# Image loads and stores of a grouped involution in halves, one to a row, behind a wait for VectorE

## The chip, the cores and the metric

The kernel runs on one core of one Trainium2 chip. The metric is the device time of one execution in microseconds (us). Every engine of the core (TensorE, VectorE, ScalarE, GpSimd, SyncE) runs its own stream of instructions in order, and semaphores order them against each other. Nearly all transfers are issued by SyncE (SP in the profile), one after the other, and are carried out by 16 DMA engines.

## The reference, cut to what matters

The input x is 8 images of 256 channels of 56 x 56, all in float32. Layer 0 adds to x an involution of its group norm; layer 1 adds a block of two 3 x 3 convolutions with ternary weights.

```python
def _L0_conv_ref(x, w_reduce, b_reduce, w_span, b_span):
    ker = jnp.einsum('bchw,oc->bohw', x, w_reduce) + b_reduce[None, :, None, None]
    ker = jnp.einsum('bchw,oc->bohw', ker, w_span) + b_span[None, :, None, None]
    ker = ker.reshape(B, G, 1, K * K, H, W)
    ...
    patches = patches.reshape(B, G, C // G, K * K, H, W)
    out = (ker * patches).sum(axis=3)
    return out.reshape(B, C, H, W)

def _L1_conv_ref(x, w1, w2, g1, b1, g2, b2):
    out1 = noised_tri_conv(x, w1)
    out1 = batch_norm_train(out1, g1, b1)
    out1 = jax.nn.relu(out1)
    out2 = noised_tri_conv(out1, w2)
    out2 = batch_norm_train(out2, g2, b2)
    return jax.nn.relu(out1 + out2)

x = x + _L0_conv_ref(_gn(x), L0_conv_w_reduce, L0_conv_b_reduce, L0_conv_w_span, L0_conv_b_span)
x = x + _L1_conv_ref(_gn(x), L1_conv_w1, L1_conv_w2, L1_conv_g1, L1_conv_b1, L1_conv_g2, L1_conv_b2)
return x
```

In layer 0 every pixel has its own 7 x 7 kernel (K = 7) for each of 16 groups of 16 channels (G = 16), and that kernel is a linear function of the pixel's own 256 channels. The change lies in layer 0.

## The kernel before

Three stages follow each other: the involution (layer 0) with its sums stored in DRAM as x1d, the two convolutions by way of y1d and y2d, and a tail that adds up and writes out. The change touches the involution alone.

**Tiling.** An image b is cut into four quarters c of 64 channels. A quarter's image tile `x` has 128 partitions: 64 channels of the upper half of the picture and the same 64 of the lower half, each with 1568 pixels. A quarter is worked on in ten rows of tiles, ty = 0 to 9, three picture rows high (the last one row high). So there are 8 x 4 x 10 = 320 rows; r = 10 c + ty counts the 40 rows of an image, and m counts the 32 quarters.

**A row.** `apply_row` multiplies on TensorE the pixel neighbourhood `q` of the row (a tile of 448 KB, read from DRAM by `load_q`) by the quarter's matrices `a`, in 56 small matmuls (L917; 28 in the last row), into `pa`. ScalarE (L927) and VectorE (L930) pick the wanted part out of it into `inv`, and GpSimd adds `inv` to x (L935). Meanwhile the matrices of the following quarter are made: `generate` yields 14 units of matmuls (L876) whose results VectorE (L890) and ScalarE (L880) move into `a`, and two steps `constant` (L845 on TensorE, L853 on VectorE). `PER_ROW` says how many of these steps a row takes: 2, 2, 2, 1, 2, 2, 2, 2, 1, 0. Rows 24 to 34 also compute the reduced kernels of the following image (`reduce`, L775, from its x tiles), and rows 4 to 18 its statistics (`gn1_stats`, L162). From row 8 of the whole on, up to about row 295, the ternary weights are made by the way: pieces of w are loaded (L319, L244) and stored again (L348, `wqd<-piece_w`) through the same SP.

**Transfers.** SP issues in the order of the text. At the start of a row stands at most one transfer of an image tile: a store of the quarter before in rows 2 and 3 (`store_x1`, L956, 64 partitions x 1568 pixels, 392 KB each), otherwise a load for the following image at the rows of `X_AT` (`load_x`, L666, 128 partitions x 784 pixels, 392 KB). Then, after `apply_row`, `prefetch` loads the `q` of five rows later into the buffer that this row has just read (`NQB` = 5), so that load waits for TensorE. GpSimd fills the rim of a `q` (L813) three rows before it is used. Tiles of x have 2 x 4 - 1 = 7 buffers. A new tile waits until its buffer's earlier tile has been read by all, the store among them.

**Order.** `pin`, at the end of every row, fixes the order of each engine's instructions to that of the text. TensorE's instructions don't change in number or order from row to row by anything said here.

Of the kernel before, what the change touches and what calls it, by code (L numbers as in the profile page):

```python
# [28 lines left out]
CH = P // 2  # L29
# [4 lines left out]
NHW = HH * W  # L34
# [27 lines left out]

PER_ROW = (2, 2, 2, 1, 2, 2, 2, 2, 1, 0)
CONST_AT = 5
NQB = 5
PLEAD = 2
RIM_AT = 1
# [31 lines left out]
def involution_tri_block_kernel(  # L99
# [3 lines left out]
    nc = tc.nc  # L103
# [6 lines left out]
    def scratch(name):  # L110
        return [[dram.tile([P, HW], F32, tag=f"{name}_{b}_{t}", name=f"{name}_{b}_{t}")
                 for t in range(CT)] for b in range(B)]

    x1_d, y1_d, y2_d = scratch("x1d"), scratch("y1d"), scratch("y2d")
# [520 lines left out]
    with ExitStack() as ph1:  # L635
# [22 lines left out]
        work = ph1.enter_context(tc.tile_pool(name="work", bufs=2))  # L658
        apool1 = ph1.enter_context(tc.tile_pool(name="apool1", bufs=1))

        def load_x(b, c, j, queue=nc.sync):

            if j == 0:
                xs[b, c] = xpool.tile([P, NHW], F32, tag="x", name=f"x_{b}_{c}")
            part = slice(j * NHW // 2, (j + 1) * NHW // 2)
            queue.dma_start(xs[b, c][:, part], x[b, c, :, part])  # L666

        def gn1_stats(b, c, j):

            if j == 0:  # L670
                gst1[c] = small.tile([P, NCB, 6], F32, tag="gn_st", name=f"st_{b}_{c}")
                if c == 0:
                    mvs[b] = small.tile([P, NCQ, 2], F32, tag="gn_mv", name=f"mv_{b}")
            image_stats(gst1[c], xs[b, c], j)
            if j == NCB - 1:
                nc.vector.bn_aggr(mvs[b][:, c, :], gst1[c].rearrange("p n s -> p (n s)"))
# [42 lines left out]
        def gn2_params(b0, b1):  # L719

            yield from group_norm_params(
                mv2[:, b0:b1].rearrange("p b t s -> p (b t) s"),
                gn2h[:, b0:b1].rearrange("p b t s -> p (b t) s"), ps_one, f"gn2_{b0}")

            for h in range(2):
                rows = slice(h * CH, (h + 1) * CH)
                nc.vector.tensor_copy(gn2[rows, b0:b1], gn2h[rows, b0:b1, h::2, :])

        gst1, mvs = {}, {}
        prm, xs = {}, {}  # L730
        for c in range(NCQ):
            for j, queue in enumerate((nc.sync, nc.scalar)):
                load_x(0, c, j, queue)
        nc.scalar.dma_start(*later.pop(0))

        def fixed(shape, name, src=None, pool=fix):
# [57 lines left out]
        def rim_of(b, c):  # L794

            sides = work.tile([P, 2, P], F32, tag="sides", name=f"sides_{b}_{c}")
            tops = work.tile([P, 3, CH], F32, tag="tops", name=f"tops_{b}_{c}")
            rim = prm[b][3][:, c]
            for dst, k0, k1, f1 in ((sides, 0, 2, P), (tops, 2, 5, CH)):
                shape = [NQ, k1 - k0, f1]  # L800
                nc.gpsimd.tensor_tensor(dst[:NQ], rims_sb[:NQ, k0:k1].unsqueeze(2).to_broadcast(shape),
                                        rim[:NQ, :f1].unsqueeze(1).to_broadcast(shape), ALU.mult)
            low = work.tile([P, CH], F32, tag="low", name=f"low_{b}_{c}")
            nc.gpsimd.tensor_copy(low[:NQ], rim[:NQ, CH:])
            around[b, c] = sides, tops, low
# [52 lines left out]
        def generate(b, c, a, shared=()):  # L858
# [5 lines left out]
            for u, (gp, p0, n) in enumerate(UNITS):  # L864
# [29 lines left out]
                yield  # L894
                if u == CONST_AT:
                    next(made)
# [3 lines left out]
        def apply_row(b, c, a, ty):  # L900


            ps = ps_a.tile([P, 512], F32, tag="pa", name=f"pa_{b}_{c}_{ty}")
            row_ps[:] = [ps]
            q = loads.pop((b, c, ty))
            whole, rest = views(a)
            if ty < TY - 1:
                av, n, t0, t1 = whole, NP, ty * TX, (TY - 1 + ty) * TX
            else:
                av, n, t0, t1 = rest, PX, 0, TX  # L910
            m = 32 if ty < TY - 1 else CH
            w = n * m * GQ // CH
            for k in range(TX):
                for h, t in enumerate((t0, t1)):
                    for g in range(CH // m):
                        o = h * CH + g * m
                        nc.tensor.matmul(ps[o:o + m, k * w:(k + 1) * w], q[:NQ, k, o:o + m],  # L917
                                         av[:, t + k, g * w:(g + 1) * w], start=True, stop=True)
            return ps, n, w // n
# [18 lines left out]
        queue = [(b, c, ty) for b in range(B) for c in range(NCQ) for ty in range(TY)]  # L938
        loads, bare, filled, around = {}, [], [], {}

        def prefetch():
            if queue:
                k = queue.pop(0)
                loads[k] = load_q(*k)
                bare.append(k)

        def surround(keep=PLEAD):
            for k in filled:
                fill_end(*k)
            filled.clear()  # L950
            while len(bare) > keep or bare and not queue:
                filled.append(bare.pop(0))
                fill_rim(*filled[-1])

        def store_x1(b, c, h):
            nc.sync.dma_start(  # L956
                x1_d[b][c // 2][c % 2 * CH:(c % 2 + 1) * CH, h * NHW:(h + 1) * NHW],
                xs[b, c][h * CH:(h + 1) * CH])

        gst = {}  # L960

        def gn2_stats(b, c, ty):

            if ty == 1:
                gst[b, c] = (small.tile([P, NCB, 6], F32, tag="gn_st2", name=f"st2_{b}_{c}"), 0)
            st, j = gst[b, c]
            while j < NCB and ((j + 1) * NC <= ty * PY * W or ty == TY):
                image_stats(st, xs[b, c], j)
                j += 1
            gst[b, c] = (st, j)  # L970
            if ty == TY:
                nc.vector.bn_aggr(mv2[:, b, c, :], st.rearrange("p n s -> p (n s)"))
# [25 lines left out]
        def matrices(m):  # L998
            return (apool if m % 2 == 0 else apool1).tile(
                [P, A_COLS], F32, tag=f"a{m % 2}", name=f"a_{m}")  # L1000

        held = []
        qpool = ph1.enter_context(tc.tile_pool(name="qpool", bufs=NQB))
        pieces = ph1.enter_context(tc.tile_pool(name="pieces", bufs=1))
# [30 lines left out]
        rim_of(0, 0)  # L1035
        for _ in range(NQB):
            prefetch()
# [9 lines left out]
        quarters = [(b, c) for b in range(B) for c in range(NCQ)]  # L1047


        X_AT = (0, 1, 4, 5, 7, 8, 14, 15)  # L1050
        PARAMS_AT = 20

        QUANT_AT = 8
        rows = [(b, c, ty) for b, c in quarters for ty in range(TY)]
# [5 lines left out]
        last = None  # L1060
        for m, (b, c) in enumerate(quarters):
            a = a_next
            gen = iter(())
            if m + 1 < len(quarters):
                a_next = matrices(m + 1)
                gen = generate(*quarters[m + 1], a_next)
            more = b + 1 < B
            for ty in range(TY):
                r = c * TY + ty

                if last is not None and ty in (2, 3):
                    store_x1(*last, ty - 2)
                elif more and r in X_AT:
                    load_x(b + 1, X_AT.index(r) // 2, X_AT.index(r) % 2)
                row = apply_row(b, c, a, ty)
                prefetch()

                if r == PARAMS_AT:
                    norm = params(b + 1) if more else gn2_params(0, b)
                next(norm, None)  # L1080

                if ty == 1 and last is not None:
                    gn2_stats(*last, TY)
                elif ty >= 2:
                    gn2_stats(b, c, ty - 1)
                for k in STATS_AT.get(r, ()) if more else ():
                    gn1_stats(b + 1, k // NCB, k % NCB)
                pick_out(b, c, ty, *row)
                surround()
                if ty == RIM_AT and m + 1 < len(quarters):  # L1090
                    rim_of(*quarters[m + 1])
                next(norm, None)
                for _ in range(PER_ROW[ty]):
                    next(gen, None)
                if more and r in STRIPS:
                    reduce(b + 1, *STRIPS[r])
                if m * TY + ty >= QUANT_AT:
                    next(quant, None)
                pin()
            for _ in gen:  # L1100
                pass
            last = b, c
# [1 line left out]
            pass  # L1104
        gn2_stats(*last, TY)
        for h in range(2):
            store_x1(*last, h)
        for _ in gn2_params(B - 1, B):
            pass

# [3 lines left out]
    with ExitStack() as ph2:  # L1114
# [36 lines left out]
        _, total = conv_phase(2, begun, y1_d, norm_y1, st2, nc2, y2_d, False, stays)  # L1151
# [4 lines left out]
    with ExitStack() as ph4:  # L1156

        h = [ph4.enter_context(tc.tile_pool(name=f"f{i}", bufs=1)) for i in range(11)]
# [27 lines left out]
        for j in range(B * CT):  # L1186
            b, t = (j // CT - 1) % B, j % CT
            n = parts_of.get(j, 1)
# [99 lines left out]
```

## Time and profile before

| | us |
|---|---|
| median of 3 runs (lowest, highest) | 2114.55 (2106.56, 2117.14) |
| the profiled execution | 2115.09 |
| its span | 2113.3 |
| involution (start to first matmul of L573) | 0 to 1033 |
| the two convolutions (L573) | 1033 to about 1900 |
| tail | about 1900 to 2113 |

Busy time in the whole span: TensorE 1744.4 us (83%), VectorE 1778.7 (84%), ScalarE 1379.2 (65%), GpSimd 463.0 (22%). Between 1100 and 1800 us TensorE is busy without a gap except at the change from the first convolution to the second. The costliest transfers of the involution, from the list of DMA issues: 320 loads of q of 448 KB each, which land a median 4.2 us after the issue; 64 loads of x of 392 KB, 5.0 us (5.4 for the 64 stores x1d of 392 KB); 64 stores of weight pieces of 144 KB, 5.2 us.

How to read the profile: PE is TensorE, PEld its loading of stationary operands, DVE VectorE, ACT ScalarE, POOL GpSimd, SP SyncE. A group names the line, the engine, the operation, out<-in and the tile. After the bar stand the total busy time and the mean in ns of one, then the idle time of the engine just before these instructions and what ended most of it. "issue" means that the profile shows nothing for which the engine waited. Lines of the waits have the total in us, the number of times and the longest one. Lines of the windows have the stretch, its length, busy time of PE, PEld, DVE, ACT and POOL with instruction counts, the granted TensorE clock, the mean busy share of the DMA engines, and GB/s. Lines of the timeline have the start, the length, engine, line and operation, and in brackets the idle time before and what ended it.

### The profile page before, as it was taken

The page shows a single profiled execution, that of the slowest core. Times are in us where ns is not written, and L with a number is a line of the kernel's source. Part 1 is how long each engine was busy: PE and PEld are TensorE (multiplying, and loading weights), DVE is VectorE, ACT ScalarE, POOL GpSimd, SP SyncE. Part 2 cuts the span into 40 slices and gives each one's busy share as a digit, 9 for nine tenths or more (in the row PEclk, how much of TensorE's full clock was granted, in tenths as well). Part 3 has the DMA queues.
Part 4 walks back from the last instruction along what each step waited for, and adds up shares of the span by engine and source line. Part 5 has one row for each costly group of instructions (what it writes and reads, how often), then busy time and mean ns, then how long its engine had stood idle before and what let it go on. Part 6 is the DMA issues. An engine that isn't in the chain of part 4 may idle for free.

```text
span 2113.3 us, 70523 instructions
## 1 busy us (share of the span) xinstructions
PE 1744.4 (83%) x29680; PEld 1612.1 (76%) x29680; DVE 1778.7 (84%) x3488; ACT 1379.2 (65%) x3413; POOL 463.0 (22%) x836
## 2 busy tenths in 40 slices
PE   5898898989889898898699999998999999990000
PEld 5786786867778786777699999998999999990000
DVE  6887879788797978878799999998999999987444
ACT  3776677766767677687467666664566666675343
POOL 1444444444444444455100000000000000000000
PEclk9999999999999999999799999999999999995555
DMA  5767778686777868677733333335234333359999
GB/s 188 226 185 230 212 202 253 185 252 202 252 216 212 244 176 256 192 212 230 269 115 135 124 123 118 124 121 196 94 125 155 125 125 125 125 213 417 430 430 396
DMA packets 154792, 433.62 MB, mean 205 GB/s; under 512 B 62942, under 2 KB 73052, under 8 KB 147564
## 3 DMA queue, kind: packets, MB, share of 16 engines
q1 hardware_dynamic: 149184, 399.08, 56.0%
q10 hardware_dynamic: 5004, 29.95, 3.4%
q8 instruction: 235, 3.85, 0.8%
q14 instruction: 81, 0.66, 0.1%
q0 software_dynamic: 288, 0.08, 0.0%
HBM read 320.07 MB, written 108.99 MB: 203 GB/s over the span
## 4 chain that ended last, share of the span: by engine, by line
PE 71%; DVE 10%; DMA 10%; issue 6%; ACT 3%; POOL 0%; ACTq 0%; SPq 0%; POOLq 0%; DVEq 0%
PE c L573 40%; PE pg L876 16%; PE pa L917 9%; DMA y1f<-y1d 7%; PE pk L775 4%; PE ks L845 2%; ACT a L880 2%; DVE a L890 1%; DMA out_y<-x1f 1%; DVE inv L930 1%; DVE st L162 1%; DVE x L853 1%; DMA wr<-in_w_red 1%; DVE y1f L1198 1%; DMA q<-in_x_nb 1%
## 5 line engine op out<-in xcount | busy, mean ns | idle before, releaser
L573 PE MATMUL c<-pl,wq 128*128 128x392 f32 x4608 | 856.9, 348 | 9.5 <-ACT pl L443 9.2
L573 PEld LDWEIGHTS c<-pl,wq 128*128 128x128 f32 x4608 | 854.9, 190 | 11.2 <-ACT pl L443 9.6
L880 ACT ACTIVATE a<-pg,bt 126x126 f32<-126x126 f32 x2028 | 519.2, 459 | 90.1 <-PE pg L876 87.1
L876 PE MATMUL pg<-kr,wl 64*126 64x140 f32 (+1 forms) x6144 | 447.9, 293 | 22.7 <-issue 17.6
L876 PEld LDWEIGHTS pg<-kr,wl 64*126 64x126 f32 x6144 | 397.4, 197 | 43.0 <-issue 19.0
L917 PEld LDWEIGHTS pa<-a,q 126*32 126x32 f32 x17024 | 237.2, 114 | 164.6 <-issue 105.7
L917 PE MATMUL pa<-a,q 126*32 126x48 f32 x17024 | 286.7, 213 | 78.9 <-issue 72.8
L890 DVE TENSOR_TENSOR a<-pg,bt 126x504 f32<-126x504 f32 (+4 forms) x640 | 278.7, 479 | 40.2 <-PE pg L876 36.8
L935 POOL TENSOR_TENSOR x<-x,inv 128x168 f32<-128x168 f32 x310 | 161.1, 520 | 520.5 <-DVE inv L930 392.1
L927 ACT ACTIVATE inv<-pa,gn1b,gn1s 128x168 f32<-128x168 f32 x320 | 163.6, 511 | 161.5 <-PE pa L917 105.2
L420 ACT CAST pl<-r 128x812 fp32r<-128x812 f32 x190 | 160.8, 867 | 130.9 <-DVE r L415 121.6
L930 DVE SCALAR_TENSOR_TENSOR inv<-pa,gn1s,inv 128x168 f32<-128x168 f32 (+1 forms) x384 | 134.0, 351 | 129.2 <-ACT inv L927 123.8
L813 POOL TENSOR_TENSOR q<-q,sides 126x256 f32<-126x256 f32 (+1 forms) x320 | 225.7, 706 | 7.3 <-DMA q<-in_x_nb 7.3
L421 DVE TENSOR_TENSOR pl<-r,pl 128x812 fp32r<-128x812 f32 x190 | 184.6, 997 | 24.9 <-ACT pl L420 23.4
L501 ACT ACTIVATE dummy<-y,nc 128x1568 f32<-128x1568 f32 (+1 forms) x128 | 200.0, 1562 | 3.0 <-DVE y L593 1.8
L396 POOL MEMSET xp<- 128x116 f32 x32 | 6.3, 197 | 829.6 <-DVE a L415 759.2
L162 DVE BATCH_NORM_STATS2 st<-x 128x6 f32<-128x392 f32 x256 | 136.9, 553 | 7.4 <-DMA x<-in_x 7.4
L1145 ACT ACTIVATE xp<-raw,bi_bn,sc_bn 128x392 f32<-128x392 f32 (+1 forms) x125 | 83.0, 721 | 60.3 <-DVE a L415 58.9
L1125 ACT ACTIVATE xp<-raw,gn 128x392 f32<-128x392 f32 (+1 forms) x125 | 83.1, 720 | 58.9 <-DVE a L415 58.9
L775 PE MATMUL pk<-x,wrn 64*128 64x168 f32 (+1 forms) x1152 | 104.1, 319 | 4.1 <-DVE x L853 2.4
L775 PEld LDWEIGHTS pk<-x,wrn 64*128 64x128 f32 x1152 | 91.5, 192 | 16.2 <-issue 9.1
L1200 DVE TENSOR_TENSOR x1f<-x1f,y1f 128x3136 f32<-128x3136 f32 (+2 forms) x22 | 55.5, 2533 | 44.2 <-DMA x1f<-x1d 37.4
(185 smaller groups left out, 1660.7 us busy)
## 6 DMA issues: line engine op xcount, KB each, us to landing
q<-in_x_nb SPq DMA_DIRECT2D x320, 448.0 KB, 4.2
raw<-x1d SPq DMA_DIRECT2D x32, 812.0 KB, 6.5
raw<-y1d SPq DMA_DIRECT2D x32, 812.0 KB, 7.2
x1d<-x SPq DMA_DIRECT2D x64, 392.0 KB, 5.4
x<-in_x SPq DMA_DIRECT2D x60, 392.0 KB, 5.0
y1d<-y SPq DMA_DIRECT2D x30, 784.0 KB, 3.3
y2d<-y SPq DMA_DIRECT2D x28, 784.0 KB, 4.0
x1f<-x1d SPq DMA_DIRECT2D x14, 1568.0 KB, 29.3
```

The costliest lines, as they stand in the source:

```text
L420: nc.scalar.copy(hi, r)
L421: nc.vector.tensor_tensor(lo, r, hi.bitcast(F32), ALU.subtract)
L501: nc.scalar.activation(dst, v, f, bias=shift[:, to:to + 1], accum_out=stats[:, to, j, n:n + 1])
L573: nc.tensor.matmul(ps[:, to, :NM], wq[k][:, t, dx, to * P:(to + 1) * P], part[:, t, :, dx:dx + W], start=(c == 0), stop=(c == last))
L775: nc.tensor.matmul(ps[h][:, :m * W], wrn[rows, c, :], src[rows, r0:r0 + (m - 1) * PY + 1:PY, :], start=(c == 0), stop=(c == NCQ - 1))
L813: nc.gpsimd.tensor_tensor(v, v, z, ALU.add)
L876: nc.tensor.matmul(dst, wl[rows, c, gp, o:o + NQ], kr[py][rows, px, :], start=True, stop=True)
L880: nc.scalar.activation(dst[:, g + 1, p0 + j], ps[1][:NQ, j * nt + t0:j * nt + t1], AF.Identity, bias=bt[:, c, g + 1, p0 + j:p0 + j + 1])
L890: nc.vector.tensor_tensor(dst[:, g, p0:p0 + n].rearrange("q p t -> q t p"), ps[0][:NQ, t0 * n:t1 * n].rearrange("q (t p) -> q t p", p=n), ...
L917: nc.tensor.matmul(ps[o:o + m, k * w:(k + 1) * w], q[:NQ, k, o:o + m], av[:, t + k, g * w:(g + 1) * w], start=True, stop=True)
L927: nc.scalar.activation(iv, parts[:, :, 0], AF.Identity, bias=prm[b][2][:, c:c + 1], scale=scale[:, 0:1])
L935: engine.tensor_tensor(xv, xv, iv.rearrange("p t (y x) -> p y t x", x=PX), ALU.add)
```

## The change

Loads and stores of an image tile are cut in halves of 64 partitions x 784 pixels (196 KB). They leave the start of the row. A new function `transfers` is called after the row's first step of `generate`: it issues the row's half and makes it wait for the last VectorE instruction that stands ahead of it in the text. Rows 1 and 2 of a quarter store the second half of the pixels (j = 1) of the quarter before, one half of the partitions (h) each. Rows 3 to 6 load the quarter six further on (`AHEAD_X`) in four pieces, the first half of its pixels first. Rows 7 and 8 store the first half of the pixels (j = 0) of this quarter: 14 picture rows, which rows ty = 0 to 4 have completed. `OPENING` places the loads of the two quarters that come before the six ahead. The second half of the last quarter is stored after the loop.

```diff
+AHEAD_X = 6
+OPENING = {(0, 0): [(4, k) for k in range(4)], (0, 1): [(5, 0), (5, 1)], (0, 2): [(5, 2), (5, 3)]}
...
-        def load_x(b, c, j, queue=nc.sync):
-
-            if j == 0:
+        def load_x(b, c, j, h=None, queue=nc.sync):
+
+            if (b, c) not in xs:
                 xs[b, c] = xpool.tile([P, NHW], F32, tag="x", name=f"x_{b}_{c}")
             part = slice(j * NHW // 2, (j + 1) * NHW // 2)
-            queue.dma_start(xs[b, c][:, part], x[b, c, :, part])
+            rows = slice(None) if h is None else slice(h * CH, (h + 1) * CH)
+            queue.dma_start(xs[b, c][rows, part], x[b, c, rows, part])
...
-        def store_x1(b, c, h):
+        def store_x1(b, c, j, h):
+            part = slice(j * NHW // 2, (j + 1) * NHW // 2)
             nc.sync.dma_start(
-                x1_d[b][c // 2][c % 2 * CH:(c % 2 + 1) * CH, h * NHW:(h + 1) * NHW],
-                xs[b, c][h * CH:(h + 1) * CH])
+                x1_d[b][c // 2][c % 2 * CH:(c % 2 + 1) * CH, h * NHW:(h + 1) * NHW][:, part],
+                xs[b, c][h * CH:(h + 1) * CH, part])
+
+        def transfers(m, ty, last):
+
+            here = nc.cur_bb.bb.instructions
+            n = len(here)
+            behind = next(i for i in reversed(here) if i.engine == mybir.EngineType.DVE).name
+            if ty in (1, 2) and last is not None:
+                store_x1(*last, 1, ty - 1)
+            if ty in (7, 8):
+                store_x1(*quarters[m], 0, ty - 7)
+            if 3 <= ty < 7 and m + AHEAD_X < len(quarters):
+                load_x(*quarters[m + AHEAD_X], (ty - 3) // 2, (ty - 3) % 2)
+            for k, piece in OPENING.get((m, ty), ()):
+                load_x(*quarters[k], piece // 2, piece % 2)
+            for i in here[n:]:
+                tc.add_manual_dep(
+                    i, behind,
+                    mybir.DependencyInfo(mybir.DependencyClass.Sync,
+                                         mybir.DependencyReason.DATA),
+                    reason="transfers in a row's middle")
...
-        X_AT = (0, 1, 4, 5, 7, 8, 14, 15)
...
-                if last is not None and ty in (2, 3):
-                    store_x1(*last, ty - 2)
-                elif more and r in X_AT:
-                    load_x(b + 1, X_AT.index(r) // 2, X_AT.index(r) % 2)
...
-                for _ in range(PER_ROW[ty]):
+                for k in range(PER_ROW[ty]):
                     next(gen, None)
+                    if k == 0:
+                        transfers(m, ty, last)
...
-            store_x1(*last, h)
+            store_x1(*last, 1, h)
```

More of the change, by code (lines that the diff above doesn't have):

```diff
@@ L732, in involution_tri_block_kernel @@
             for j, queue in enumerate((nc.sync, nc.scalar)):
-                load_x(0, c, j, queue)
+                load_x(0, c, j, queue=queue)
         nc.scalar.dma_start(*later.pop(0))
```

## Prediction

> **What bounds the kernel now.** I read the page first, then the windows, the waits, one stretch of the timeline, and the packet and instruction records of the trace. From the page, the chain that ended last, three groups and one queue:
>
> ```profile
> PE 71%; DVE 10%; DMA 10%; issue 6%; ACT 3%; POOL 0%; ACTq 0%; SPq 0%; POOLq 0%; DVEq 0%
> ...
> L917 PEld LDWEIGHTS pa<-a,q 126*32 126x32 f32 x17024 | 237.2, 114 | 164.6 <-issue 105.7
> L917 PE MATMUL pa<-a,q 126*32 126x48 f32 x17024 | 286.7, 213 | 78.9 <-issue 72.8
> ```
>
> ```profile
> q8 instruction: 235, 3.85, 0.8%
> ```
>
> TensorE sets the time. The change touches only the involution, which ends at 1033 us; the convolutions after it are TensorE at 100% and the tail is the DMA engines, so only the first 1033 us can move. There TensorE loses time ahead of L917, to "issue", a wait for nothing that the profile names. The windows cut image 3 (rows 0 to 16, 17 to 24, 25 to 39 of its 40):
>
> ```profile
> 427.60:484.40 56.80, 46.01 (x1306) 38.38 (x1304) 47.18 (x137) 36.64 (x136) 24.96 (x45) 0.91 0.80 251
> 484.40:507.10 22.70, 20.58 (x602) 17.31 (x600) 21.75 (x66) 14.87 (x58) 11.75 (x21) 0.92 0.78 243
> 507.10:551.10 44.00, 43.41 (x1206) 37.57 (x1204) 31.44 (x72) 36.98 (x135) 19.99 (x35) 1.00 0.59 181
> ```
>
> The first pair of numbers after the length is TensorE busy; the last two are DMA share and GB/s. In the first 17 rows TensorE is idle 10.8 of 56.8 us, with the DMA engines at 0.80; in the last 15 it is idle 0.6 of 44.0, at 0.59. Image 5 says the same (8.4 idle of 53.7 at 0.86, 0.5 of 44.2 at 0.61). The waits of the first and third of these windows:
>
> ```profile
> PEld pa L917 <- issue: 11.9, 8, 3.4
> PE pa L917 <- issue: 10.2, 8, 3.2
> ```
>
> ```profile
> PEld pa L917 <- issue: 2.0, 8, 0.7
> PE pa L917 <- issue: 0.5, 1, 0.5
> ```
>
> One such wait in the timeline:
>
> ```profile
> 470.17 1.23 SPq L348 DMA_DIRECT2D wqd<-piece_w  x1
> ...
> 473.85 0.34 SPq L666 DMA_DIRECT2D x<-in_x  x1
> ...
> 474.31 0.36 SPq L790 DMA_DIRECT2D q<-in_x_nb  x1
> ...
> 475.00 0.32 SPq L666 DMA_DIRECT2D x<-in_x  x1
> ...
> 477.83 0.49 PE L917 MATMUL pa<-a,q 126*32 126x48 f32 x15 [3.23 <-issue]
> ```
>
> SP issued 392 + 448 + 392 KB within 1.5 us; TensorE then stood still 3.23 us in the middle of a row's 56 matmuls, where no operand can be late. What was late is its instructions. The trace has 235 packets of 16,384 bytes on queue 8. Counting TensorE's records, 29 of its 35 idle gaps over 1 us between 50 and 1030 us begin at one place modulo 256 records, and it resumes about 1.3 us after such a packet ends. So I take a block as asked for when TensorE enters the one before it. Here that was at 471.27; the packet started 3.88 us later, took 1.19, and TensorE went on 1.50 us after. Over 195 blocks from row 0 on, the gaps at block starts sum to 86.3 us. By region, and by whole image transfers (x or x1d) issued from 3 us before to 1.5 us after the request (requests; mean stall):
>
> - rows 0 to 16: none 28, 0.43 us; one 38, 0.74; two 17, 1.21. Sum 60.5 us.
> - rows 17 to 24: none 26, 0.17; one 11, 0.34; two 1, 1.57. Sum 9.7 us.
> - rows 25 to 39: none 58, 0.05; one 10, 0.25; two 2, 0.27. Sum 5.9 us.
> - the last ten rows before the convolution: 4 requests, 10.2 us.
>
> [...] the mean time to its start is 1.36 us with no image transfer near, 2.24 with one, 3.12 with two. [...] No run here shows halves yet; the argument rests on when they are issued, not on their running side by side.
>
> **The change, part by part.** *Bytes* stay. Mean packet times give the load on each engine: a q load 8 packets of 3,584 bytes x 188 ns = 1.5 us; a whole x load 8 x 142 = 1.14; a whole store 4 x 310 = 1.24; a half 4 x 142 = 0.57 (estimate).
>
> *Spread.* Before, the rows of an image carry 8 loads at rows 0, 1, 4, 5, 7, 8, 14, 15 and stores at rows 2, 3 of each quarter: 12 of 16 whole transfers in 17 rows. After, rows 1 to 8 of each quarter carry one half: 14 halves, the bytes of 7 transfers, in rows 0 to 16; 6 against 2 transfers (4 halves) in rows 17 to 24; 12 halves against 4 in rows 25 to 39.
>
> *First estimate, per request.* A half is worth half a step of the list. A request spans about 4.5 us, one row and a half; with 8 of 10 rows carrying a half I take no, one, two halves at 0.15, 0.50, 0.35. Rows 0 to 16: 0.15 x 0.43 + 0.50 x 0.585 + 0.35 x 0.74 = 0.62, x 83 = 51 us, against 60.5. Rows 17 to 24: 0.27 x 38 = 10, against 9.7. Rows 25 to 39: 0.17 x 70 = 12, against 5.9. Net -3 us.
>
> *Second estimate, by load.* The no-transfer class itself is worse in the loaded rows (0.43 against 0.05), so backlog reaches past my window. Stall per request is 0.73, 0.25 and 0.08 us in the three regions, with DMA shares near 0.83, 0.72 and 0.60; evened to some 0.73, about 0.28 x 191 requests = 53 us, against 76. That is -23, flattered by rows 25 to 39, whose strip matmuls use instructions more slowly. I take the middle of both, -13.
>
> *The new wait.* SP waits for the row's last VectorE instruction after the first unit, nearly always an L890 (or an L853). Queued behind it are the weight pieces and the next q load. Measured in the trace of before, that end lies 1.3 to 3.9 us after the row's last L917; against the end of the next row's L917, which the next q load awaits anyway, it is 0.8 us earlier on the mean in rows 5 to 7 but about even in rows 0, 1 and 3 and 0.7 later in row 2 (worst 4.9). A q load is issued five rows ahead and filled by GpSimd two rows after, so it has some 6 us, of which landing takes 4.2. GpSimd now waits 7.3 us in all for q; I take 1 us of harm, 0 to 25.
>
> *Loads six quarters ahead.* Seven buffers hold x, so quarter m+6 reuses that of m-1, whose last half is stored in row 2 of m: the first load, in row 3, waits for that landing (5.4 us for a whole store, against rows of 3). SP stands 1 to 3 us in each of 26 quarters; before it stood 19.2 us in 7 such waits. The q load behind it has the slack just named. The last quarter's pieces (rows 15, 16) are due at the statistics of row 18, about 3.6 us of VectorE later for a landing of some 4: up to 1 us in 7 images, mostly VectorE's own slack. Taken 2 us, 0 to 7.
>
> *SP's issues.* 120 more at 0.43 to 0.61 us, some 60 us, inside the 629.9 us that it waits for TensorE:
>
> ```profile
> SPq L790 <- PE pa L917: 629.9, 286, 21.0
> ...
> SPq L666 <- DMA x1d<-x: 19.2, 7, 5.6
> ```
>
> If SP's queue is held as above, that cover is thinner just in rows 0 to 3.
>
> *The seam.* In the built order the first load of the convolution moves ahead of the last rows' q loads, and half of the last stores leave earlier, so 812 KB less stand at 1013 us before the 5.28 us fetch stall at 1018; taken -2, between -4 and +3. The sum is -13 + 1 + 2 - 2 = -12. VectorE, 83 to 96% busy in rows 0 to 24, is next in line and may take some of it back. The profiled execution is 2115.1 us (span 2113.3 and 1.8 around it), 0.5 above the median shown: about 2103.
>
> **Rivals.** (a) *Moved, not removed*: the first estimate holds, the stalls reappear in rows 25 to 39. For it: the steps are almost linear in the number of transfers. Against it: the base differs by region. 2111. (b) *Slower, by q*: the wait for VectorE stands in front of q loads. From the point where SP is held over about 4 us beyond the next row's L917, GpSimd's fill and then L917 wait. Such lags occur in rows 2 and 3 of quarters that also quantize; if two thirds of the 32 quarters lose 1.2 us each, +25 on the forecast: 2128. Against it: two rows of slack. (c) *Far better*: every row becomes like 25 to 39, 0.08 x 191 = 16 us of stall, -60; VectorE's load lets about half through: 2083. (d) That the halves don't go out apart: the built order shows one half between q loads in rows 1 to 8, apart from the opening, so only the first load of a quarter, held by its store, can bunch.
>
> **How the numbers follow.** Forecast 0.45, (a) 0.27, (b) 0.16, (c) 0.12. A measurement of this kernel tells 0.5%, 10.6 us, from no change. The forecast's own spread (2096 to 2109) lies over this bound for about three quarters and within it for the rest; (a) is within, but for a little over it on the slow side; (b) slower; (c) faster. Faster 0.34 + 0.12 = 0.46; same 0.11 + 0.25 = 0.36; slower 0.16 + 0.02 = 0.18. The range takes in the forecast, (a), the nearer half of (c) and the beginnings of (b): 2084 to 2121, with some 0.19 left out.
>
> **What would show it.** Right: the idle time ahead of L917 in rows 0 to 16 falls by some 15 us over the images while that of rows 25 to 39 rises by a few; the DMA share is near 0.7 in all three windows; no image transfer stands within 0.5 us of another. Wrong: L813 or L917 waits for q's landing (b); the sum of "issue" ahead of L917 is unchanged (a); or TensorE's freed time comes back as waits for L890's output.

## The result, and the profile after

The changed kernel takes 2125.22 us in the median of 16 runs (2113.28 to 2132.41), the kernel before 2112.24 us in 16 runs on the same chip (2104.16 to 2122.27). The ratio of the runs is 1.005, 95% interval 1.0031 to 1.007: about 11 us slower, where 12 us faster was forecast. (This ratio and those below are not quotients of the medians, which would be 1.006 here.) Its profiled execution (2113.28 us, span 2111.5) happens to be the fastest of its 16, so it doesn't show the loss. Its lines are therefore read beside those of a second profile of the same kernel (2122.26 us, span 2120.5), which comes with the first experiment. Line numbers have moved: L917 of before is L920, L890 is L893, L790 is L793, L666 is L669, L956 is L960, L162 is L164, L324 is L326.

The page of the changed kernel, the chain by engine and two groups of step 5:

```profile
PE 67%; DVE 12%; DMA 12%; issue 5%; ACT 3%; POOL 1%; SPq 0%; ACTq 0%; POOLq 0%; DVEq 0%
...
L920 PEld LDWEIGHTS pa<-a,q 126*32 126x32 f32 x17024 | 236.5, 114 | 152.8 <-issue 90.2
...
L164 DVE BATCH_NORM_STATS2 st<-x 128x6 f32<-128x392 f32 x256 | 137.8, 553 | 16.5 <-DMA x<-in_x 16.3
```

The chain has moved from TensorE (71% to 67%) to VectorE and the DMA engines (10% to 12% each). The wait for instructions ahead of L920's weight loads fell from 105.7 to 90.2 us, but in the second profile it is 111.4:

```profile
L920 PEld LDWEIGHTS pa<-a,q 126*32 126x32 f32 x17024 | 236.5, 114 | 166.6 <-issue 111.4
```

Two profiles of one kernel differ by 21 us here, so a single profile's "issue" doesn't settle a question of 10 us. The part of this loss that is a wait for instructions is called a fetch stall below. In the changed kernel 27 of TensorE's 39 idle gaps over 1 us between 50 and 1030 us begin at one place modulo 256 records (29 of 35 before), and after these TensorE resumes a mean 1.45 us after a packet of 16,384 bytes on queue 8 ends (1.38 before). The prediction's 1.36, 2.24 and 3.12 us are mean times from a block's request, as it takes it, to the start of that packet. Summed at the starts of the instruction blocks, as in the prediction, the fetch stalls are (rows 0 to 16, 17 to 24, 25 to 39, last ten rows): before 60.5 + 9.7 + 5.9 + 10.2 = 86.3 us; after 46.1 + 6.3 + 8.6 + 10.4 = 71.4; second profile 53.4 + 10.8 + 12.0 + 9.0 = 85.1.

SP issues in the order of the text: in the trace of the kernel before, each of the 118 image transfers that the rows issue stands between the same two q loads as in the text. The waits of SyncE's queue in the whole span, changed kernel:

```profile
SPq L960 <- DVE a L893: 198.9, 89, 5.3
SPq L793 <- PE pa L920: 164.2, 121, 20.6
SPq L669 <- DVE a L893: 80.6, 66, 4.0
```

Before, SP stood 629.9 us waiting for TensorE ahead of the q loads. That has fallen to 164.2, and 279.5 us of waiting for VectorE's L893 alone stand ahead of the halves. SP is now held more by VectorE than by TensorE. The waits of VectorE between 50 and 1025 us, in the second profile:

```profile
DVE st L164 <- DMA x<-in_x: 15.4, 9, 3.5
...
DVE piece_w L326 <- DMA piece_w<-in_w: 3.7, 7, 0.8
```

Before, VectorE waited for no transfer in this stretch. Now it waits for image pieces (L164, the statistics of the next image) and for weight pieces (L326). All nine waits of L164, and all eight in the first profile, lie in VectorE's rows 16 and 18 of an image, counted from the order of the instructions: there it takes the statistics of the next image's last quarter, whose halves are loaded in rows 13 to 16. TensorE in turn waits for what VectorE makes next. Before, and in the changed kernel (11.7 us in both of its profiles):

```profile
PE pg L876 <- DVE a L890: 3.7, 7, 1.2
```

```profile
PE pg L879 <- DVE a L893: 11.7, 15, 2.6
```

The windows of image 3 in the changed kernel, cut at the same rows as before (columns as before, DMA share and GB/s last):

```profile
429.80:482.00 52.20, 44.34 (x1304) 36.86 (x1300) 46.54 (x134) 36.80 (x137) 24.86 (x44) 0.93 0.81 227
482.00:508.10 26.10, 20.67 (x605) 16.91 (x605) 22.48 (x68) 14.87 (x58) 11.68 (x21) 1.00 0.77 221
508.10:554.70 46.60, 44.99 (x1233) 38.85 (x1232) 33.39 (x75) 38.37 (x135) 20.99 (x37) 1.00 0.79 225
```

The spread did what it says for the bytes: 227, 221, 225 GB/s instead of 251, 243, 181. But the DMA share evened out at 0.79, not at 0.73: rows 0 to 16 stay where they were (0.80) and rows 25 to 39 rise from 0.59. Rows 0 to 16 became 4.6 us shorter and rows 17 to 24 3.4 us longer; of the 2.6 us that the last window is longer, one is that before's ends 1 us ahead of the row's end.

### The profile page after: what moved, and what is told of

Its sections match the earlier page's. It is cut to its first block, busy times and chain, and to the rows that moved or that the text cites. A ratio compares the mean times of both kernels' runs of the same rounds, so it can differ in the third digit from the quotient of the medians.

```text
span 2111.5 us, 70809 instructions
## 1 busy us (share of the span) xinstructions
PE 1744.2 (83%) x29680; PEld 1608.9 (76%) x29680; DVE 1779.4 (84%) x3488; ACT 1380.4 (65%) x3413; POOL 462.6 (22%) x836
## 4 chain that ended last, share of the span: by engine, by line
PE 67%; DVE 12%; DMA 12%; issue 5%; ACT 3%; POOL 1%; SPq 0%; ACTq 0%; POOLq 0%; DVEq 0%
PE c L575 39%; PE pg L879 14%; PE pa L920 8%; DMA y1f<-y1d 7%; PE pk L778 4%; PE ks L848 2%; DVE a L893 2%; ACT a L883 2%; DMA out_y<-x1f 1%; DMA x<-in_x 1%; DVE st L164 1%; DVE inv L933 1%; DVE x L856 1%; DMA piece_w<-in_w 1%; DMA wr<-in_w_red 1%
## 5 line engine op out<-in xcount | busy, mean ns | idle before, releaser
L920 PEld LDWEIGHTS pa<-a,q 126*32 126x32 f32 x17024 | 236.5, 114 | 152.8 <-issue 90.2
L920 PE MATMUL pa<-a,q 126*32 126x48 f32 x17024 | 285.1, 212 | 67.3 <-issue 61.4
L893 DVE TENSOR_TENSOR a<-pg,bt 126x504 f32<-126x504 f32 (+4 forms) x640 | 278.1, 479 | 32.9 <-PE pg L879 29.4
L933 DVE SCALAR_TENSOR_TENSOR inv<-pa,gn1s,inv 128x168 f32<-128x168 f32 (+1 forms) x384 | 133.8, 350 | 114.8 <-ACT inv L930 109.7
L164 DVE BATCH_NORM_STATS2 st<-x 128x6 f32<-128x392 f32 x256 | 137.8, 553 | 16.5 <-DMA x<-in_x 16.3
```

What stands on the lines that cost most here:

```text
L893: nc.vector.tensor_tensor(dst[:, g, p0:p0 + n].rearrange("q p t -> q t p"), ps[0][:NQ, t0 * n:t1 * n].rearrange("q (t p) -> q t p", p=n), ...
```

## The experiments

Each ratio below compares a kernel's runs with those of the kernel before on the same chip, and its 95% interval follows. Waits are from one profile each, between 50 and 1025 us. The short names (e1, e2 and so on) stand for the kernels in what follows. In the expectations, "theory H" and its rivals are the guesses at the cause that a run was to tell apart.

### The wait, and the spread without it

**The changed kernel again** (e1), unchanged, gave the second profile and a level to compare with.

> The changed kernel unchanged, for a second profile, since its profiled execution (span 2111.5 us) lies at the fast end of its runs (2113 to 2132). Theory H (held queue): SP's wait for VectorE holds the q loads, weight pieces and image pieces queued behind it, and TensorE and VectorE lose what the shorter fetch stalls gain; then a profile of a typical length (near 2123) shows fetch stalls near 71 us at the block starts as before, but more idle time on VectorE ahead of L164, L250 and L326 (DMA) and on GpSimd ahead of L816 (q) than the 16 + 7 + 15 us of the first profile. Rival F (fetch): the typical run differs from the fast one in its fetch stalls, which rise back to 86 us or more. Time against before: 1.003 to 1.007.

1.0061 (1.0043 to 1.0079). The typical run's fetch stalls came out at 85.1 us, nearly as rival F said, and L164's waits rose from 9.1 to 15.4 us, as H said. So this run alone doesn't decide between the two.

**Without the wait** (e2). The half follows the row's q load at once.

```diff
-            for i in here[n:]:
-                tc.add_manual_dep(
...
-                    reason="transfers in a row's middle")
```

> Halves, rows and six quarters ahead as in the changed kernel, the wait for VectorE taken away: a half goes out right behind the row's q load. H: the q load's lag behind L920 falls back from 1.5 to about 0.5 us, and the time falls to 0.992 to 0.998 of before, the gain of the spread alone. Rival F: the halves now stand back to back with q, bursts of 644 KB in 8 of 10 rows, fetch stalls over 86 us, 1.005 or slower. Rival W (six quarters ahead: the store's landing held in front of the first load, and the pieces late for the statistics): no change from the changed kernel, 1.003 to 1.007.

1.0005 (0.9991 to 1.002). The loss is gone, which speaks against F and W, but the gain of 0.2 to 0.8% that H expected of the spread isn't there. Fetch stalls in this profile are 94.5 us, more than before's 86.3, at the same time as before.

**Without the wait, at the row's start** (e3), where the kernel before has its transfers; halves, rows and six quarters' lead are those of the change.

```diff
+                transfers(m, ty, last)
                 row = apply_row(b, c, a, ty)
                 prefetch()
...
-                    if k == 0:
-                        transfers(m, ty, last)
```

> As e2_no_wait, but the half stands at the start of the row in the text, ahead of its q load, where the kernel before has its whole transfers. H: as e2, 0.992 to 0.998, within 0.002 of it; image pieces one row earlier for the statistics. F: 1.005 or slower. W: 1.003 to 1.007.

0.9991 (0.9976 to 1.0006), here too less than H expected. Stalls by region 56.6 + 9.2 + 11.8 + 7.4 = 84.9 us: 4 us less in rows 0 to 16, 6 us more in rows 25 to 39.

**The wait alone** (e4). The kernel before, with its whole transfers in its own rows, moved behind the row's first unit and made to wait for VectorE.

```diff
-                if last is not None and ty in (2, 3):
-                    store_x1(*last, ty - 2)
-                elif more and r in X_AT:
-                    load_x(b + 1, X_AT.index(r) // 2, X_AT.index(r) % 2)
...
+                    if k == 0:
+                        here = nc.cur_bb.bb.instructions
+                        n = len(here)
+                        behind = next(i for i in reversed(here) if i.engine == mybir.EngineType.DVE).name
+                        if last is not None and ty in (2, 3):
+                            store_x1(*last, ty - 2)
+                        elif more and r in X_AT:
+                            load_x(b + 1, X_AT.index(r) // 2, X_AT.index(r) % 2)
+                        for i in here[n:]:
+                            tc.add_manual_dep(
...
```

> The kernel before with whole transfers in its own rows, only moved to behind the row's first unit and made to wait for VectorE: the wait alone. H: slower than before, 1.003 to 1.010, SP holding q loads in 16 of 40 rows. F: faster or equal (0.995 to 1.000), since the transfers no longer stand back to back with q. W: equal to before, 0.999 to 1.001.

1.0054 (1.0033 to 1.0074). So the wait makes the loss: the change without it is level with before (e2, e3), and before with it loses about as much as the change. Nor do fetch stalls look like the loss: they are 73.6 us here, less than before's, and 94.5 in e2, which loses nothing. The waits of VectorE and TensorE in this kernel, which has no halves:

```profile
DVE st L162 <- DMA x<-in_x: 10.0, 8, 2.1
DVE piece_w L324 <- DMA piece_w<-in_w: 9.5, 7, 3.1
```

```profile
PE pg L876 <- DVE a L890: 18.2, 14, 4.2
```

TensorE waited 3.7 us for L890 before.

### When the awaited instruction ends

**An earlier instruction** (f3). The half waits for the last VectorE instruction of `pick_out`. In the changed kernel's trace it ends 0.9 us before the one that the change awaits, in the mean of the rows (0.6 to 1.5 us by row), not the 2 us that the expectation took.

```diff
                 pick_out(b, c, ty, *row)
+                behind = next(i for i in reversed(nc.cur_bb.bb.instructions)
+                              if i.engine == mybir.EngineType.DVE).name
```

> The changed kernel, but the half waits for the last VectorE instruction of pick_out (L933 in most rows), which stands ahead of the row's first unit and ends about 2 us earlier than that unit's L893; the place in SP's order is unchanged. V and Q: SP is freed before the next row's L920, VectorE's waits for loads fall under 6 us, 0.999 to 1.003. If the wait as such costs (theory S, a semaphore wait on VectorE in SP's queue, whenever it ends): 1.004 to 1.008.

1.001 (0.9991 to 1.0028). Most of the price is gone, though SP issues a half only 0.85 us earlier: 0.70 us after the row's last `pick_out` instruction in the mean, against 1.55 in the changed kernel. But VectorE's waits for transfers, which V expected under 6 us, are still 12.0.

**The wait in some rows only**: `for i in here[n:] if ty >= 5 else ()` (g1), and the reverse (g2).

> The changed kernel with the wait kept only in rows 5 to 8 of a quarter (the second half of the loads, the first half of the stores), where the awaited VectorE instruction ended 0.7 to 1.1 us ahead of the next row's last L917 in the kernel before; rows 0 to 4 have no wait. Theory H (the price comes from rows in which the awaited instruction ends beyond the next row's L920, so that SP stands in front of q loads, weight pieces and image pieces): 0.999 to 1.002, VectorE's waits for loads under 8 us. Theory S (each wait costs, wherever): half the price, 1.002 to 1.004.

> The opposite: the wait kept only in rows 0 to 4. H: the whole price, 1.004 to 1.007, with VectorE's waits for weight pieces as in the changed kernel. S: 1.002 to 1.004.

Waiting in rows 5 to 8 alone 1.0034 (1.0017 to 1.0051), in rows 0 to 4 alone 1.0083 (1.0055 to 1.0111). The early rows carry the larger part, as the measured lags of the prediction say, but the late ones are not free: g1 lies in the range of theory S, not of H, and g2 above both. The two parts together (1.2%) are more than the whole (0.5 to 0.6%), so the price isn't a sum over rows.

**GpSimd's queue** (f4). The same halves and the same wait, issued by GpSimd (`nc.gpsimd.dma_start`), so that q loads and weight pieces have SP to themselves.

> The changed kernel with all its halves issued by GpSimd instead of SP, behind the same wait, so that nothing of SP's is held; GpSimd pays about 0.55 us for each issue, as its first DMAs show, with 22% of its time in use. V: weight pieces arrive in time, image pieces may still be late for the statistics (up to 10 us of waits), 1.000 to 1.004. Q: 0.998 to 1.001. If making the transfers later is itself harmful, 1.004 or more.

1.0082 (1.0058 to 1.0107), slower than every range expected but the last. The wait now stands ahead of GpSimd's own filling and adding. GpSimd stands 20.5 us for L893 ahead of its stores, and VectorE waits longer for image pieces:

```profile
DVE st L164 <- DMA x<-in_x: 25.8, 11, 4.5
```

### Who waits for what the held queue brings

**Six buffers for q** (g3; `NQB` 5 to 6), so that every q load leaves a row earlier.

> The changed kernel with six q buffers instead of five: every q load goes out one row earlier, so a held SP leaves it a row more. Theory Q (the price comes through late q tiles: GpSimd waits for them, ScalarE's copy L829 for GpSimd): GpSimd's wait for q falls from 19 to 20 us to under 8, ScalarE's for GpSimd from 24 to about 10, and the time to 0.998 to 1.002. Theory V (through the late pieces on VectorE): 1.004 to 1.007, VectorE's waits for loads still 15 to 20 us.

1.0083 (1.0052 to 1.0114). GpSimd's waits for q fell from 15 to 4.2 us (7.3 before the change), and the loss stayed. So late q tiles don't make the loss, unless the sixth buffer has a price of its own; the kernel before wasn't run with six. Lines of the changed kernel's second profile and of this one:

```profile
POOL q L816 <- DMA q<-in_x_nb: 15.1, 13, 4.7
```

```profile
POOL q L816 <- DMA q<-in_x_nb: 4.2, 7, 1.4
```

VectorE still waited:

```profile
DVE st L164 <- DMA x<-in_x: 13.8, 11, 2.4
DVE piece_w L326 <- DMA piece_w<-in_w: 8.5, 8, 2.6
```

**Statistics and weight steps one row later**, to give their loads more time, in the changed kernel (f1) and, as a control, in the kernel before (f2).

```diff
-STATS_AT = {r: (r - 4,) for r in range(4, 18)} | {18: (14, 15)}
+STATS_AT = {r: (r - 5,) for r in range(5, 19)} | {19: (14, 15)}
...
-            for n, f in ((0, fetch), (2, ternary), (3, planes_of), (5, store)):
+            for n, f in ((0, fetch), (3, ternary), (4, planes_of), (6, store)):
```

> The changed kernel, wait and all, with VectorE's own uses of what SP loads put one row later: the statistics of the following image (row r uses piece r-5 instead of r-4) and the three steps of a weight piece behind its load. Theory V (VectorE, nearly full, waits for the image and weight pieces that the held SP brings late, some 16 to 21 us in all in three profiles with the wait, against 0 to 2 without): these waits fall under 6 us, TensorE's wait for L893 from 12 to about 4 us, and the time to 0.999 to 1.003 of before. Rival Q (the loss is in the q loads held behind the transfer): 1.004 to 1.008, as the changed kernel.

> Control: the kernel before with the same uses one row later and nothing else. V and Q both: 0.998 to 1.002, since VectorE waits there for no such load; any shift is the price or gain of the other order itself, to be taken off f1_later_after.

1.0068 (1.0044 to 1.0091) and 1.0037 (1.0021 to 1.0053). The edit has a price of its own: the statistics now end too close to row 20, where TensorE needs them, as the control's waits show:

```profile
PE pa L169 <- DVE mv L676: 12.1, 7, 2.7
```

The changed kernel loses 1.0068 / 1.0037 = 1.0031 against its control, and the two intervals leave room for nearly nothing as well as for nearly the full price. VectorE's waits for image and weight pieces did go (0.4 us are left), as theory V expected, and no return of the time to before's level can be seen. It decides little, and doesn't support V.

**The weight piece first** (g4). The half stands behind the row's weight transfers in SP's queue, and the wait is the same.

```diff
                 if m * TY + ty >= QUANT_AT:
                     next(quant, None)
+                if PER_ROW[ty]:
+                    transfers(m, ty, last, behind)
```

> The changed kernel with the half put behind the row's weight transfer in SP's order, the wait being the same: the weight pieces of a row are no longer held by its own wait, q loads and image pieces are as before. If the weight pieces carry the price: 1.000 to 1.003 and VectorE's wait for them under 2 us. Otherwise 1.004 to 1.007.

1.0031 (1.0018 to 1.0045): about half of the price. L326's waits are gone from the trace, and L164's stay (9.8 us).

**Both dependences taken away.** `gn1_stats` of every image but the first reads 392 columns of a constant tile instead of the image piece: VectorE does the same work and doesn't wait for the load. These kernels leave out the true statistics of seven images. First in the changed kernel (h1), then with the weight piece first as well (h2), then, as the control, in the kernel before (h3).

```diff
-            image_stats(gst1[c], xs[b, c], j)
+            if b == 0:
+                image_stats(gst1[c], xs[b, c], j)
+            else:
+                nc.vector.bn_stats(gst1[c][:, j, :],
+                                   wl.rearrange("p c g w -> p (c g w)")[:, :NC])
```

> The changed kernel, but the statistics of the images that are loaded during the involution (L164 called from the rows, eight images less the first) read 392 columns of a constant tile instead of the loaded piece: as many VectorE instructions of the same shape, and no wait of VectorE for an image piece. The numbers of those normalizations are therefore not the images'. Theory V (VectorE waits for image and weight pieces that the held queue brings late): the waits of L164 for the loads, 9 to 15 us in the changed kernel, are gone, those for weight pieces (4 to 5 us) stay; ratio to before 1.001 to 1.004. Theory O (the held transfers cost through something other than VectorE's waits): no change, 1.006 plus or minus 0.0015.

> As h1, and with the row's weight piece issued ahead of the held half, as in g4 (which gave 1.0031 by itself): no wait of VectorE for either kind of piece. Theory V: the level of the control h3, 1.000 plus or minus 0.0015, and VectorE waits for DMA under 3 us. Theory O: g4's 1.0031 again, although VectorE waits for no DMA.

> Control: the kernel before with the same statistics of a constant tile. Before had no wait of VectorE for an image piece, so both theories expect 1.000 plus or minus 0.001; what it departs from that is the price of the edit itself, to be taken off h1 and h2.

1.004 (1.0023 to 1.0056), 0.9997 (0.9978 to 1.0016), and 1.0001 (0.998 to 1.0022) for the control. With image pieces and weight pieces both free of the held queue, the wait costs nothing that can be measured, though it stands in the same rows behind the same instruction. Freed of one kind alone it still costs 0.3 to 0.4%, and h1's interval overlaps that of the changed kernel. So under this wait the loss needs VectorE's dependence on what SP, held for VectorE, brings late. All of VectorE's waits for transfers in h2:

```profile
DVE xp L1154 <- DMA raw<-x1d: 1.0, 1, 1.0
DVE piece_w L326 <- DMA piece_w<-in_w: 0.2, 1, 0.2
```

How VectorE's waits become lost time is not shown by their totals. TensorE's wait for VectorE's L893 (L897 in h2) is 9.0 us in h2, which loses nothing, and 9.5 in g4, which does. And f3 and two kernels of the next part (h4 and i2) lose little or nothing, although VectorE waits there as long for image pieces as in kernels that lose.

### What the change can give once its wait is cheap

**Both mends at once** (h4): weight piece first, and the wait for `pick_out`'s last VectorE instruction.

> The changed kernel with both mends: the half stands behind the row's weight piece in the queue, as in g4, and waits for the last VectorE instruction of the row's pick_out, about 2 us earlier, as in f3. f3 gave 1.001 and kept 12 us of VectorE's DMA waits. Theory V: 0.998 to 1.000, the level of e3 (0.9991), since the wait then costs nothing and the spread gains 1 to 2 us at most. If the spread of the loads were worth what the prediction took (13 us): 0.994 to 0.996. Theory O: f3's 1.001.

0.997 (0.9955 to 0.9986), 2108.5 us in the median of 22 runs against 2115.43: faster than both kernels, a little more than the level foreseen. Two more kernels ask which part brings this: the same order without the wait (i1), and the same order and wait with the whole transfers of before (i2).

> The changed kernel without the wait for VectorE (as e2), the half standing behind the row's weight piece in the queue (as in g4). If the cheap wait is worth something by itself (it keeps a half from starting with the row's own q load): e2's and e3's level, 0.999 to 1.0005. If the spread with the weight piece first is what gains: h4's 0.997 or below.

> The kernel before with its whole transfers in its own rows, moved behind the row's weight piece and waiting for the last VectorE instruction of pick_out, as in h4: both mends, but no halves and no six quarters. If the spread and the lead are what gains: 1.000 plus or minus 0.0015. If the place in the row and its wait gain, whatever is moved: h4's 0.997.

1.0002 (0.9984 to 1.0019) and 1.0011 (0.9995 to 1.0027). Neither part shows a gain alone; the halves with a cheap wait do, about 6 us. The interval of i1 touches that of h4, and its medians (2107.48 against 2110.27 us) would give 0.9987, so a gain from the wait itself is possible and not shown. That h4 is ahead of whole transfers under the same wait stands clear; i2 lacks the halves, their rows and the six quarters' lead, so which of these gains is open. VectorE's waits for image pieces in h4 and in i2:

```profile
DVE st L164 <- DMA x<-in_x: 8.1, 7, 1.8
```

```profile
DVE st L162 <- DMA x<-in_x: 14.0, 7, 3.0
```

## Why the prediction was wrong, by its steps

**"The new wait ... I take 1 us of harm, 0 to 25."** This is the step that failed. It measured 11 to 15 us (0.54% alone in e4; 0.56 and 0.70% between the changed kernel run again and e2 or e3), inside the bounds and far from the value taken. The working looked only at q loads, which have two rows of slack; g3 speaks against q. It named the weight pieces as queued behind the wait and gave them no price; keeping them out of the wait is worth about half of the loss (g4). And the halves themselves, which wait longest, were priced only under the six quarters' lead, as "up to 1 us in 7 images, mostly VectorE's own slack", where VectorE waited 9 to 15 us, all of it at those pieces. VectorE's slack was the wrong cover: it is 83 to 96% busy in rows 0 to 24 of image 3, and TensorE needs its L893 next. Of the prediction's own signs of being wrong, the last one came: TensorE's wait for L893 (L890 of before) rose from 3.7 to 11.7 us.

The timeline of the changed kernel's second profile shows how one such loss can come about; the rows are counted from the order of the instructions (start and length in us; the idle time before in brackets):

```profile
474.00 0.37 DVE L933 SCALAR_TENSOR_TENSOR inv<-pa,gn1s,inv 128x168 f32<-128x168 f32 x1
...
474.98 0.45 SPq L960 DMA_DIRECT2D x1d<-x  x1
...
476.16 1.68 SPq L793 DMA_DIRECT2D q<-in_x_nb  x1
...
478.89 0.49 SPq L669 DMA_DIRECT2D x<-in_x  x1
...
480.76 2.00 SPq L669 DMA_DIRECT2D x<-in_x  x1
...
487.50 0.57 DVE L164 BATCH_NORM_STATS2 st<-x 128x6 f32<-128x392 f32 x1 [3.55 <-DMA x<-in_x]
...
488.28 1.26 DVE L893 TENSOR_TENSOR a<-pg,bt 126x504 f32<-126x504 f32 x2
...
489.01 1.15 PE L879 MATMUL pg<-kr,wl 64*126 64x126 f32 x16 [2.62 <-DVE a L893]
```

TensorE had finished row 12 at about 469, but VectorE came to that row's L933 only at 474.00, so the store of row 12 left at 474.98, and the q load of row 13, queued behind it, was reached 3.3 us after row 13's own matmuls. The loads of rows 13 and 14 followed at 478.89 and 480.76, the first of them once the store had landed and its buffer was free; SP was done with the second only at 482.76. VectorE needed both in row 16 and stood 3.55 us; L893 was late by that; TensorE stood 2.62 us for L893. A VectorE that is behind delays the transfers that it will itself wait for. That is how a wait can cost what it does with all buffers in place. That every one of the losses is of this form isn't shown, and the totals of single profiles don't order the kernels: VectorE's waits for transfers are 12.0 us in f3 (1.001), 8.1 in h4 (0.997) and 14.5 in i2 (1.0011), against 9.8 in g4 (1.0031).

**The spread, -13 us, as the middle of two estimates.** The first estimate, per request (-3), came nearer: e3, the spread without the wait, gave 0.9991, -2 us, with an interval from -5 to +1. Its regions came out at 56.6, 9.2 and 11.8 us where the estimate had 51, 10 and 12, so their sum, 77.6 us, is not below the 76.1 of before; that the stalls bring the -2 isn't shown. (The totals of the changed kernel's two profiles differ by 14 us.) The second estimate (-23) took it that the DMA share would even out at some 0.73. It evened out at 0.79, since the same bytes kept the DMA engines busy for longer. The list of queues between 50 and 1025 us, in the kernel before:

```profile
q1 hardware_dynamic: 119897, 211.10, 71.5%
```

and in the changed kernel:

```profile
q1 hardware_dynamic: 125952, 211.57, 76.2%
```

The same bytes cost 4.7% of 975 us more, 46 us on each of the 16 engines. In this kernel it lies in the image's packets: 3,136 bytes took 196 ns in the mean, where the prediction reckoned with 142, so a half took 4 x 196 = 0.78 us per engine instead of 0.57; the q packets kept their time (186 against 188 ns). In other kernels the times of packets that are under way together shift against each other: with the halves alone (e3) the image's packets took 169 ns and the q packets 195, with the wait alone (e4) a whole store's packets of 6,272 bytes 398 instead of 310 and the q packets 179. So only the queue's total is compared: 697 us per engine in the kernel before, 731 with the halves alone (e3), 703 with the wait alone (e4), 743 with both. Most of the rise comes with the halves, little with the wait. So the halves kept the engines busier than the whole transfers, and without the wait they gained nothing that can be measured (0.9991, 0.9976 to 1.0006, in e3).

**Six quarters ahead, +2 us; SP's issues, nothing; the seam, -2.** No run took these apart. In e3 all of them together with the spread come to -2 us, so their sum is not far off; errors that cancel would not show. The wait for a store's landing ahead of a quarter's first load came as reckoned: 25 times and 41.4 us in the changed kernel. In e3 it is 39.3 us, and the time is level with before, so this holding of SP has no price that shows. The stalls of the last ten rows, where the seam was to gain, are 10.4 and 9.0 us in the changed kernel's two profiles against 10.2.

**The rivals.** (a), moved and not removed, was right about the spread: no gain that can be measured. (b), slower by the held queue, had the right sign and by luck nearly the right time (2128), since its path led by q, GpSimd and L917, against which g3 speaks. (c), far better, didn't come. (d) didn't come either: between 70 and 1020 us no two halves left within 0.5 us of each other in either profile. What should have been asked of every transfer queued behind the wait was who uses it next and with how much slack; the answer for two of the three kinds was VectorE itself.

## What to carry to other kernels

A wait put on a queue that issues in order, as SP's does here, holds everything behind it (the q load of row 13 above was reached 3.3 us after its row's matmuls): list each of these transfers with its next user and that user's slack, and be most careful where the user is the engine waited for, since its own lag then comes back to it. If transfers must be paced, wait for the earliest instruction that does the pacing, and put what has little slack ahead of the wait; here these two moves turned +0.6% into -0.3%, although the earlier instruction ended only 0.9 us sooner. Before loads are moved from crowded to idle stretches in smaller pieces, measure what the pieces cost: here the same bytes kept the DMA queue busy 5% longer (731 against 697 us), and the spread alone gained nothing that could be measured.

## What else the runs showed

Near a long fetch stall the granted clock is often at half. The timeline of the kernel before, after the stall shown in the prediction:

```profile
477.83 0.49 PE L917 MATMUL pa<-a,q 126*32 126x48 f32 x15 [3.23 <-issue]
478.26 3.51 PE L876 MATMUL pg<-kr,wl 64*126 64x126 f32 x32
```

32 matmuls of this form took 3.51 us, where they take 2.03 elsewhere:

```profile
485.12 2.03 PE L876 MATMUL pg<-kr,wl 64*126 64x126 f32 x32
```

The trace's record of the granted clock has 21 stretches at 0.5 between 50 and 1035 us of the kernel before, 102 us in all, of which 20 are 3.4 or 6.8 us long and the last 20.5; one begins at 477.9, where the stall just shown ends. At 16 of the 21, a fetch stall of more than 1 us ends between 2.2 us before the stretch begins and 0.9 us after; these stalls last 1.3 to 3.3 us. That the stalls bring the stretches is not shown. In a stretch one matmul of L876 follows the other after 112 ns (median of 16 groups of 16), outside after 59 (302 groups). So what a stretch costs shows as TensorE busy and not as idle, and no sum in the prediction had counted that. It doesn't explain the loss: the changed kernel has 17 stretches with 82 us in its fast profile and 15 with 72 us in the slower one.
